# Layer 0 of a two-layer transformer: values' projection one unit later, two gate transposes earlier, and another order of the last two batches' normalisations and expert choices

## The chip, the cores and the metric

The kernel runs on one core of one Trainium2 chip. A core has five engines with a queue of instructions each: TensorE (PE in the profile, its weight loads PEld), VectorE (DVE), ScalarE (ACT), GpSimd (POOL) and SyncE (SP), which issues transfers. They wait for one another by semaphores. The metric is the device time of one execution in microseconds, lower is better; times shown are medians of several runs. The profile is one further execution; its times are counted from the start of its span.

## The reference, cut to what matters

Eight sequences (batches) of 256 tokens of 128 features pass through two layers. Each layer is an attention and a mixture of experts, both behind a normalisation that is modulated per sequence:

```
h = layernorm(x) * (1 + ca) + sa
x = x + ga * attention(h, W_qkv, b_qkv, W_out, b_out)     # 16 heads of 8, causal
h = layernorm(x) * (1 + cb) + sb
logits = h @ Wr                                           # 8 experts, the best 2 of each token
x = x + gb * (shared_ffn(h) + sum over the token's 2 experts of gate * expert_ffn(h))
```

The modulations (sa, ca, ga, sb, cb, gb) are linear in a small input. The shared feed-forward network and each expert have a hidden width of 512. Layer 1 is alike, with other sizes; the change touches layer 0 alone.

## The kernel before, in words

The order of the work is written out by hand: each engine runs its instructions in the order in which the program states them, and waits only on data and on buffers. Around the loops stand tables of steps: `at(n, ...)` puts a step into unit n ahead of its value products, `at_end(n, ...)` at the unit's end, and `at_head(n, half, ...)` behind the exponential of one of its two halves. Steps of one list run in the order in which they were registered.

**Attention of layer 0.** The loop runs over 24 units n = 3b + u, three for each batch b. `scores0(b, u)` (L1117, L1129) makes transposed scores on PE into two PSUM buffers "s", ACT takes their exponentials into `pt` (L1133), and for u = 0 and 1 POOL clears what lies above the diagonal (`causal`, L820). Two units later `values0` (L1151) multiplies `pt` with the values `vm`. In unit u = 1 the next batch is projected: `project0(b+1)` (L1081; ACT writes k and four scaled queries, L1084 and L1086) and `project_v0(b+1)` (vp on PE, L1095; the addition of the bias on DVE, L1098, writes `vm`). When a batch's three units are through, `normalise0(b)` (DVE, L1161 to L1171: transpose, reciprocal, multiplication, transpose back, giving aT) and, a unit later, `finish0(b)` (y on PE, L1184, added to x on DVE, L1187) close it.

All small products (qk, vp, y, nt, lg, rk, gp) share two PSUM buffers with the tag "p".

**Routing of layer 0.** It runs in six spans of batches, (0,1), (2,3), 4, 5, 6, 7, most of it inside the attention loop. For a span, `norm0` gives four steps: measure (statistics on DVE, L748 to L753, and a power on POOL, L754), normalise (xn on DVE, L764), modulate (nt on PE, L773; h on DVE, L782) and tokens (two multiplications on POOL, L1209 and L1210). `route0` is cut into steps as well: the logits lg (PE, L1231) and the best expert (DVE, L848 to L855); the second best and the counts (DVE, L848 to L912); the ranks rk (PE, L915 to L918) and the row numbers idx (DVE, L920 to L926); and then one scatter for each half batch and choice, so four for a batch (POOL, L930). A scatter writes 128 tokens into the experts' rows `xs` in DRAM. A small memset (L1388) stands ahead of each, in `scatter(go, times)`. The last scatter of all waits until all the others have landed and stands for them.

**The end of the stage.** After the loop a written-out list finishes batch 7, the routing of batches 5 to 7, and the shared network of the four wide tiles w (512 tokens each): `hides` are the hidden products (L1264, gelu on ACT, L1267), `projects` the outputs (ysh, L1288), four token groups for each w, of which the last product adds the experts' biases with the gates turned to rows (L1292). `turn_gates0(w)` makes those: a transpose on PE (gp, L1274) and a copy on DVE (gT, L1276). The gates of the first two wide tiles are computed in units 19 and 21. Then SyncE reads each expert's rows (`fetch_rows0`, xg, L1321), and 39 expert tiles follow (L1327 to L1350), for which POOL gathers weights by index (L1047).

Of the kernel before, what the change touches and what calls it, by code (L numbers as in the profile page):

```python
# [17 lines left out]
B, S = 8, 256  # L18
# [539 lines left out]
def fast_path(ctx: ExitStack, tc: tile.TileContext, i: dict, out: bass.AP, bad: bass.AP):  # L558
# [19 lines left out]
    def ps_ln(shape, name):  # L578
        return pp.tile(shape, F32, tag="p", name=name)
# [97 lines left out]
    def modulation(n):  # L677
        mp = ps_ln([P, 7, B], f"mp{n}")
        for k, what in enumerate((SA, CA, GA, SB, CB, GB)):
            nc.tensor.matmul(  # L680
                out=mp[:, what, :], lhsT=wmod[n][:, bass.ts(k, P)], rhs=silu_c[n], start=True, stop=True
            )
        m = md[n]
        nc.vector.tensor_copy(m[:, SA:, :], mp[:, SA:, :])
        nc.vector.tensor_scalar_add(m[:, CA, :], m[:, CA, :], 1.0)
        nc.vector.tensor_copy(m[:, 0:BG, :], mp[:, 0:BG, :])
# [116 lines left out]
    def batch_cols(tiles, b):  # L803
        return tiles[b * S // TW][:, bass.ds(b * S % TW, S)]

    def batch_tokens(b):
        return x[b // 2][:, bass.ts(b % 2, 2), :]
# [264 lines left out]
    SPANS0 = ((0, 2), (2, 2), (4, 1), (5, 1), (6, 1), (7, 1))  # L1072
# [18 lines left out]
    def project_v0(b):  # L1091
        hb = batch_cols(h, b)
        vp = ps_ln([P, 2, P], f"vp0_{b}")
        for j in range(2):
            nc.tensor.matmul(  # L1095
                out=vp[:, j, :], lhsT=hb[:, bass.ts(j, P)], rhs=wqkv[:, bass.ts(2, P)], start=True, stop=True
            )
        nc.vector.tensor_tensor(  # L1098
            vm[b % 3].rearrange("p k a (m c) -> p k (a m) c", m=2)[:, :, :, 0:D0],
            vp.rearrange("p k (h d) -> p k h d", d=D0),  # L1100
            bv.rearrange("p (h d) -> p h d", d=D0).unsqueeze(1).to_broadcast([P, 2, H, D0]), ALU.add,
        )
# [54 lines left out]
    def normalise0(b):  # L1157

        o = st0.pop(("o", b))
        ot = ap0.tile([P, 2, S // 32, 32], F32, tag="ot", bufs=1, name=f"ot0_{b}")  # L1160
        nc.vector.transpose(ot.rearrange("p s k c -> p (s k c)"), o.rearrange("p s q -> p (s q)"))  # L1161
        r = rs0[:, b]
        nc.vector.reciprocal(r, ot[:, :, :, 16:18])
        at = ap0.tile([P, S // 32, 2, 2, D0], F32, tag="t", name=f"at0_{b}")
        for s in range(2):
            nc.vector.tensor_tensor(
                at[:, :, s], ot[:, s, :, 0:16].rearrange("p k (m d) -> p k m d", m=2),
                r[:, s].unsqueeze(3).to_broadcast([P, S // 32, 2, D0]), ALU.mult,
            )
        aT = ap0.tile([P, S], F32, tag="aT", name=f"aT0_{b}")  # L1170
        nc.vector.transpose(aT, at.rearrange("p k s m d -> p (k s m d)"))  # L1171
        st0["aT", b] = aT
# [5 lines left out]
    def finish0(b):  # L1178
        aT = st0.pop(("aT", b))
        xb = batch_tokens(b)  # L1180
        shape = [P, 2, P]
        y = ps_ln(shape, f"y0_{b}")
        for j in range(2):
            nc.tensor.matmul(  # L1184
                out=y[:, j, :], lhsT=aT[:, bass.ts(j, P)], rhs=mdb0[:, GA - 1, b, :], start=True, stop=True
            )
        nc.vector.tensor_tensor(xb, xb, y, ALU.add)  # L1187
# [11 lines left out]
    def norm0(bs):  # L1199

        kept = []
        name = f"0b{bs[0]}"

        def tokens():
            b, half = bs[0] // 2 * 2, bs[0] % 2
            if not half:
                tokens0["all", b] = ap0.tile([P, 4, P], F32, tag="ht", bufs=2, name=f"ht{name}")
            ht = tokens0[bs] = tokens0["all", b][:, bass.ds(2 * half, 2 * bs[1]), :]
            nc.gpsimd.tensor_tensor(by_batch(ht), by_batch(kept[0]), rows_of_span(mdb0[:, CB - 1], bs), ALU.mult)  # L1209
            nc.gpsimd.tensor_tensor(by_batch(ht), by_batch(ht), rows_of_span(mdb0[:, SB - 1], bs), ALU.add)  # L1210

        first = 2 * (bs[0] % 2)
        return [
            *layernorm_parts(
                bs[0] // 2, md[0], SB, CB, name, ps_ln, lambda w, xn: kept.append(xn),
                range(first, first + 2 * bs[1]),
            ),
            tokens,
        ]

    def route0(bs):

        nt = 2 * bs[1]
        first = 2 * bs[0]
        ts = bass.ds(first, nt)
        name = f"0_{bs[0]}"
        shape = [P, nt, E0]
        lg = ps_ln(shape, f"lg{name}")
        for j in range(nt):
            c = bass.ts((first + j) % TT, P)  # L1230
            nc.tensor.matmul(out=lg[:, j, :], lhsT=h[bs[0] // 2][:, c], rhs=wr, start=True, stop=True)  # L1231
        s = z0.s12[:, ts]
        yield from top2_steps(ap0, lg, s, g12[:, ts], name, -1e30)
        yield from z0.place_steps(first, nt, lambda: tokens0[bs], ps_ln)
# [37 lines left out]
    def turn_gates0(w):  # L1272
        gp = ps_ln([P, P], f"gp0_{w}")
        nc.tensor.transpose(gp, gates[:, bass.ts(w, TT), :].rearrange("p j e -> p (j e)"), ident)  # L1274
        gT = hid0["g", w] = ap0.tile([P, P], F32, tag="gT", bufs=2, name=f"gT0_{w}")
        nc.vector.tensor_copy(gT, gp)  # L1276
# [97 lines left out]
    def at(n, *steps):  # L1374
        early.setdefault(n, []).extend(steps)

    def at_end(n, *steps):
        ends.setdefault(n, []).extend(steps)
# [5 lines left out]
    def one(steps):  # L1384
        return lambda: next(steps, None)

    def apart_on_gpsimd():
        nc.gpsimd.memset(most, P - 0.5)  # L1388

    def scatter(go, times):  # L1390
        for _ in range(times):
            apart_on_gpsimd()
            go()

    N0 = 3 * B
    at_end(3, lambda: modulation(1))
    at_end(4, lambda: normalise0(0))
    at_end(5, lambda: scale_wout(), lambda: add_bias(0), lambda: add_bias(1))
# [11 lines left out]
            at_end(n + 1, lambda w=w: add_bias(w))  # L1410
        at_end(n + 3, modulate)
    at(6, lambda: finish0(0))
    for b in range(1, B - 1):
        at_end(3 * b + 4, lambda b=b: normalise0(b))
        at_end(3 * b + 5, lambda b=b: finish0(b))
    ways = {}
    spots = {
        0: ((13, 1), (14, 0), (14, 0), (14, 1), (16, 1), (17, 0), (17, 0), (17, 1)),
        2: ((19, 1), (20, 0), (20, 0), (20, 0), (20, 1), (21, 0), (21, 1), (21, 1)),
        4: ((22, 1), (22, 1)), 5: (),  # L1420
    }
    for bs in SPANS0[:4]:
        n = 3 * sum(bs) + 2
# [12 lines left out]
    at_end(19, first_gates)  # L1436
    at(21, first_gates)
    norm6, norm7 = norm0(SPANS0[4]), norm0(SPANS0[5])
    at_end(23, norm6[0], lambda: ways[SPANS0[3]]())

    project0(0)
    project_v0(0)
# [12 lines left out]
    def set_up():  # L1455
        rd0 = rows_of(0, md[0])
        spread(mdb0, rd0, GA, 4)
        spread(gb0.unsqueeze(1), rd0, GB, 1)
        w1.update({n: load(w1p, n, nc.sync) for n in ("wo1", "gate_w", "wg1", "wu1", "wd1")})
        for n in range(2):  # L1460
            nc.sync.dma_start(out=wds1[bass.ts(n, I1), :], in_=i["wds1"])
        nc.sync.dma_start(out=gate_b, in_=i["gate_b"].partition_broadcast(P))
        nc.sync.dma_start(out=bp32, in_=i["bp32"])
        z0.clear(zero)
        z1.clear(zero)
        for e in range(E0 - 3):
            wst.append(ap0.tile([P, WPK], F32, bufs=1, name=f"wst{e}"))
            nc.sync.dma_start(out=wst[e], in_=i["wpk"][bass.ts(e, P), :])
        nc.gpsimd.memset(gates, 0.0)
        nc.gpsimd.memset(gates[:, :, E0 : E0 + 1], 1.0)  # L1470

    rd1 = []

    for n in range(N0):
        b, u = divmod(n, 3)
        scores0(b, u, behind.pop(n, {}))
        if n == 0:
            set_up()
        if u == 1 and b + 1 < B:
            project0(b + 1)  # L1480
            project_v0(b + 1)
        for step in early.pop(n, ()):
            step()
        if n > 1:
            values0(*divmod(n - 2, 3))
        for step in ends.pop(n, ()):
            step()


    go4, go5 = ways[SPANS0[2]], ways[SPANS0[3]]  # L1490
    go6, go7 = one(route0(SPANS0[4])), one(route0(SPANS0[5]))

    hides = [one(shared_hidden_steps0(w)) for w in range(3)]
    projects = [one(shared_project_steps0(w)) for w in range(3)]
# [5 lines left out]
    go5()  # L1500
    normalise0(B - 1)
    norm6[2]()
    scatter(go4, 2)
    scatter(go5, 4)
    for n in range(len(wst), E0):
        fetch_weights0(n)
    hides[0]()
    finish0(B - 1)
    norm7[0]()
    go6()  # L1510
    norm6[3]()
    norm7[1]()
    go6()
    turn_gates0(0)
    projects[0]()
    norm7[2]()
    go7()
    go6()
    scatter(go6, 4)
    projects[0]()  # L1520
    norm7[3]()
    go7()
    projects[0]()
    projects[0]()
    go7()
    scatter(go7, 4)
    hides[1]()
    last_gates()
    one(shared_add0(0))()
    turn_gates0(1)  # L1530
    hides[1]()
    for n in range(6):
        fetch_rows0(n)
# [517 lines left out]
    for n in range(N):  # L2051
        b, u = divmod(n, 4)
# [22 lines left out]
    go6, go7 = (one(route1((b, 1))) for b in (B - 2, B - 1))  # L2075
# [206 lines left out]
```

## Time and profile before

| What | Value |
|---|---|
| Time, median of 3 runs | 606.93 us (605.57 to 607.95) |
| The profiled execution: its time, its span | 603.21 us, 601.5 us |
| Mean granted TensorE clock | 0.967 |
| PE busy | 539.9 us (90%) |
| DVE, ACT, POOL busy | 330.9, 268.1, 263.0 us |
| Attention loop of layer 0, PE's first scores to its last y in the loop | 14.1 to 111.4 us |
| End of the stage: last scatter landed, first expert row turned on PE | 146.56, 150.41 us |
| First unit of layer 1's attention on PE | about 247 us |

Four views are used below. The chain that ended last follows the last instruction back to what released it, step by step; its lines give start, length and what ran, and "issue" is time in which the engine waited for nothing that the view shows. The waits give who waited for whom: microseconds in total, how often, the longest. The timeline gives the start and the length of an engine's instructions in order of time, merged where alike follow one another, with the idle time ahead of them and what ended it in brackets. The stage view gives each engine's busy time and the granted TensorE clock in a stretch of the span. [...]

### The profile page before, as it was taken

To read this page: it belongs to the slowest core of one execution; us is meant where nothing else is said; L and a number is where in the kernel's file an instruction comes from. 1 tells how busy PE (TensorE), PEld (TensorE's weight loads), DVE (VectorE), ACT (ScalarE), POOL (GpSimd) and SP (SyncE) were. 2 spreads that over 40 slices of the span, in tenths; PEclk is the share of its full clock that TensorE was granted. 3 is DMA by queue.
4 is the path that set the end of the run, shared out by engine and by line. 5 is a ranking of instruction groups with operands and counts; after the bars stand their busy time and mean duration, and the time that the engine had idled before them with its cause. 6 is when DMAs were issued, how large, how long until landed. Compare 5 with 4: busy or idle time off the path is not lost.

```text
span 601.5 us, 11911 instructions
## 1 busy us (share of the span) xinstructions
PE 539.9 (90%) x4443; PEld 383.3 (64%) x4443; DVE 330.9 (55%) x1005; ACT 268.1 (45%) x486; POOL 263.0 (44%) x404
## 2 busy tenths in 40 slices
PE   5998999867999999899999999999999989888960
PEld 4454454554999998666676767676766757764450
DVE  4257776864422222465535765655647495654693
ACT  3686666403455563275334442445262542522430
POOL 5323578846044442375612354633065553104750
PEclk9998999979899999899999999999999999888996
DMA  8799994402289992410403031300303036563441
GB/s 274 275 402 404 390 355 168 142 19 79 89 263 319 342 309 74 161 28 19 94 5 72 11 81 23 81 23 3 71 20 88 14 86 195 170 190 77 104 103 59
DMA packets 53567, 85.41 MB, mean 142 GB/s; under 512 B 6652, under 2 KB 32764, under 8 KB 52348
## 3 DMA queue, kind: packets, MB, share of 16 engines
q1 hardware_dynamic: 45308, 60.50, 31.5%
q0 software_dynamic: 8048, 23.67, 12.8%
q8 instruction: 37, 0.61, 0.4%
q10 hardware_dynamic: 144, 0.39, 0.2%
q14 instruction: 30, 0.25, 0.1%
HBM read 53.46 MB, written 31.07 MB: 141 GB/s over the span
## 4 chain that ended last, share of the span: by engine, by line
PE 60%; DVE 13%; DMA 10%; ACT 5%; issue 5%; POOL 5%; SPq 1%; POOLq 0%; DVEq 0%; ACTq 0%
PE sc L1641 7%; PE o L1663 6%; PE qp L1610 5%; PE hp L1336 5%; PE yt L1344 4%; PE kp L1610 4%; PE y L1716 4%; PE vp L1623 4%; PE sc L1117 4%; PE sum L1671 3%; DMA wt<-in_wpk_dram,widx 3%; POOL xs L930 3%; PE o L1151 2%; DMA xg<-xs 2%; ACT pt L1133 1%
## 5 line engine op out<-in xcount | busy, mean ns | idle before, releaser
L820 POOL TENSOR_SCALAR_AFFINE_SELECT pt<-pt 128x256 f32<-128x256 f32 (+1 forms) x144 | 67.2, 494 | 152.6 <-ACT pt L1644 116.3
L1055 POOL DMA_INDIRECT yg<-ys,yidx x56 | 54.3, 970 | 52.1 <-DMA ys<-ysb 34.0
L1644 ACT ACTIVATE pt<-sc 128x768 f32<-128x768 f32 x64 | 48.4, 808 | 25.8 <-PE sc L1641 25.7
L1133 ACT ACTIVATE pt<-sc 128x1024 f32<-128x1024 f32 x48 | 46.5, 1023 | 24.8 <-PE sc L1117 15.5
L1641 PEld LDWEIGHTS sc<-q,k 64*128 64x128 f32 x512 | 41.6, 187 | 18.8 <-issue 13.9
L1338 ACT ACTIVATE hst<-hp,wt 128x128 f32<-128x128 f32 x136 | 38.9, 368 | 29.7 <-ACT hst L1338 20.1
L1047 POOL DMA_INDIRECT wt<-in_wpk_dram,widx x31 | 29.0, 935 | 50.3 <-PE xT L1327 49.7
L1641 PE MATMUL sc<-q,k 64*128 64x256 f32 (+1 forms) x512 | 50.5, 336 | 0.0
L1663 PE MATMUL o<-pt,v 128*64 128x256 f32 (+1 forms) x512 | 49.0, 332 | 1.3 <-DVE ou L1675 1.3
L1626 ACT COPY v<-vp 128x512 f32<-128x512 f32 x32 | 18.8, 586 | 67.0 <-PE vp L1623 67.0
L1614 DVE COPY q<-qp 128x512 f32<-128x512 f32 x32 | 22.0, 688 | 39.9 <-PE qp L1610 39.9
L1663 PEld LDWEIGHTS o<-pt,v 128*64 128x64 f32 x512 | 32.0, 136 | 18.5 <-POOL pt L820 5.3
L1349 DVE COPY ysb<-yt 128x128 f32<-128x128 f32 x39 | 11.4, 292 | 54.9 <-PE yt L1344 54.9
L1610 PE MATMUL qp<-h,wq 128*128 128x256 f32 x128 | 36.8, 411 | 2.8 <-DVE q L1614 1.4
L930 POOL DMA_INDIRECT xs<-ht0b,idx x32 | 32.2, 1005 | 15.0 <-issue 12.0
L1336 PE MATMUL hp<-xTs,wt 128*128 128x128 f32 x272 | 36.7, 278 | 1.9 <-DMA wt<-in_wpk_dram,widx 1.4
L1117 PE MATMUL sc<-qm,k 32*128 32x512 f32 x192 | 35.9, 702 | 2.1 <-ACT pt L1133 1.5
L1623 PE MATMUL vp<-wv,h 128*128 128x512 f32 x64 | 36.1, 646 | 0.0
L1344 PE MATMUL yt<-wt,hst 128*128 128x128 f32 x272 | 35.8, 275 | 0.0
L1336 PEld LDWEIGHTS hp<-xTs,wt 128*128 128x128 f32 x272 | 33.0, 191 | 3.7 <-issue 1.6
L1610 PE MATMUL kp<-h,wk 128*128 128x256 f32 x128 | 33.7, 387 | 0.0
L1614 ACT COPY k<-kp 128x512 f32<-128x512 f32 x32 | 18.8, 588 | 33.3 <-PE kp L1610 33.3
(298 smaller groups left out, 1088.7 us busy)
## 6 DMA issues: line engine op xcount, KB each, us to landing
xs<-zero SPq DMA_DIRECT2D x1, 12288.0 KB, 58.3
xs<-zero SPq DMA_DIRECT2D x1, 8192.0 KB, 25.3
rb<-rd SPq DMA_DIRECT2D x14, 512.0 KB, 5.9
mdb<-mrd SPq DMA_DIRECT2D x2, 2048.0 KB, 7.3
xg<-xs SPq DMA_DIRECT2D x63, 64.0 KB, 3.0
wt<-in_wpk_dram SPq DMA_DIRECT2D x24, 128.0 KB, 2.6
wst<-in_wpk_dram SPq DMA_DIRECT2D x5, 514.0 KB, 12.4
ys<-ysb SPq DMA_DIRECT2D x10, 256.0 KB, 3.2
```

The costliest lines, as they stand in the source:

```text
L820: nc.gpsimd.affine_select(out=pt, in_=pt, compare_op=ALU.is_ge, fill=0.0, base=0, pattern=[[0, pt.shape[1]], [1, P]], channel_multiplier=-1,)
L930: self.apart(nc.gpsimd.indirect_dma_start(out=self.xs[:, :], out_offset=bass.IndirectOffsetOnAxis(ap=idx[:, j, k : k + 1], axis=0), in_=to ...
L1055: nc.gpsimd.indirect_dma_start(out=yg[:, k, :], out_offset=None, in_=self.ys[:, :], in_offset=bass.IndirectOffsetOnAxis(ap=self.yidx[:, j, ...
L1117: nc.tensor.matmul(out=sc[:, n, :].rearrange("p (a q) -> p a q", q=rhs.shape[2]), lhsT=k[r, cols], rhs=rhs, start=True, stop=u < 2,)
L1133: nc.scalar.activation(pt[:, bass.ts(half, 2), :], sc, AF.Exp)
L1336: nc.tensor.matmul(out=hp[:, c, :], lhsT=wt[:, bass.ts(c, P)], rhs=xT, start=True, stop=True)
L1344: nc.tensor.matmul(out=y, lhsT=hs[:, c, :], rhs=wt[:, bass.ds(WF + c * P, P)], start=(c == 0), stop=(c == FC - 1))
L1610: nc.tensor.matmul(out=ps_[:, n, :], lhsT=w1[f"w{what}1"][:, bass.ts(2 * u + n, P)], rhs=hb, start=True, stop=True)
L1623: nc.tensor.matmul(out=vp, lhsT=hb[:, bass.ts(j, P)], rhs=w1["wv1"][:, bass.ts(half, 512)], start=True, stop=True)
L1641: nc.tensor.matmul(out=sc[:, n, cols], lhsT=k[r, m, bass.ts(kb, P)], rhs=q[r, m, qs], start=True, stop=True)
L1644: nc.scalar.activation(pt, sc[:, :, 0:384], AF.Exp, scale=1.0 / math.sqrt(D1))
L1663: nc.tensor.matmul(out=o[bass.ts(n, D1), m, qs], lhsT=v[:, kb, bass.ts(4 * (u % 2) + 2 * m + n, D1)], rhs=pts[m][:, n, cols], start=(kb == ...
```

## The change

Four things differ in layer 0; the operations themselves, their sizes and their number are the same.

- The values of batch b are projected in its own first unit (n = 3b) instead of the unit 3b − 2. Queries and keys stay where they were.
- `normalise0(b)` and `finish0(b)` of batches 1 to 6 are registered first, so they lead the lists of units 7, 10 and 13 instead of standing behind the modulation's last steps and the addition of the bias.
- The gates of wide tiles 0 and 1 are turned at the end of unit 23, not within the shared network's products. All four scatters of batch 4 stand in units 22 and 23, not two of them.
- In the written-out end, batch 6's tokens come ahead of batch 5's scatters; batch 7's power stands ahead of the last of these; batch 6's choice, ranks and scatters come ahead of batch 7's modulation and choice; the shared network's outputs are spread between them in another way.

```diff
     N0 = 3 * B
+    for b in range(1, B - 1):
+        at_end(3 * b + 4, lambda b=b: normalise0(b))
+        at_end(3 * b + 5, lambda b=b: finish0(b))
     at_end(3, lambda: modulation(1))
...
     at(6, lambda: finish0(0))
-    for b in range(1, B - 1):
-        at_end(3 * b + 4, lambda b=b: normalise0(b))
-        at_end(3 * b + 5, lambda b=b: finish0(b))
     ways = {}
     spots = {
...
-        4: ((22, 1), (22, 1)), 5: (),
+        4: ((22, 0), (22, 1), (22, 1), (23, 0)), 5: (),
     }
...
-    at_end(23, norm6[0], lambda: ways[SPANS0[3]]())
+    at_end(23, norm6[0], lambda: turn_gates0(0), lambda: turn_gates0(1), lambda: ways[SPANS0[3]]())
...
         if u == 1 and b + 1 < B:
             project0(b + 1)
-            project_v0(b + 1)
+        if u == 0 and b:
+            project_v0(b)
...
     normalise0(B - 1)
     norm6[2]()
-    scatter(go4, 2)
-    scatter(go5, 4)
+    norm6[3]()
+    scatter(go5, 3)
     for n in range(len(wst), E0):
         fetch_weights0(n)
     hides[0]()
     finish0(B - 1)
     norm7[0]()
+    scatter(go5, 1)
     go6()
-    norm6[3]()
+    projects[0]()
+    go6()
     norm7[1]()
+    projects[0]()
     go6()
-    turn_gates0(0)
+    scatter(go6, 4)
     projects[0]()
     norm7[2]()
     go7()
-    go6()
-    scatter(go6, 4)
-    projects[0]()
-    norm7[3]()
-    go7()
-    projects[0]()
     projects[0]()
     go7()
+    norm7[3]()
+    hides[1]()
+    go7()
     scatter(go7, 4)
-    hides[1]()
     last_gates()
     one(shared_add0(0))()
-    turn_gates0(1)
     hides[1]()
```

## The prediction

> **What bounds the kernel now.** I read the chain that ended last first, then the waits of the two stretches that the change touches, then each engine's timeline there. "Unit n" is the n-th pass of the 24-pass attention loop; b is a batch. The chain shows that the end of layer 0's routing hangs on GpSimd's scatters:
>
> ```profile
> 123.94 0.05 POOL most L1388
> 123.99 7.45 issue
> 131.44 1.06 POOL xs L930
> ...
> 144.34 2.23 DMA xs<-ht0b,idx
> ...
> 147.43 6.11 DMA xg<-xs
> ```
>
> GpSimd (POOL) stands 7.45 us before batch 6's first scatter; then eight scatters follow, the last lands at 146.56, and only then SyncE may read the experts' rows (xg). What POOL waited for is VectorE's (DVE) row numbers, and behind what those stood, the timelines of DVE and PE tell:
>
> ```profile
> 122.48 1.57 DVE L764 TENSOR_SCALAR xn0b<-x,mv0b,rstd0b 128x128 f32<-128x128 f32 x2 [0.89 <-POOL rstd0b L754]
> ...
> 125.46 0.28 DVE L1276 COPY gT<-gp 128x128 f32<-128x128 f32 x1
> ...
> 130.50 0.17 DVE L926 CAST idx<-slot 128x4 int32<-128x4 f32 x1
> ```
>
> ```profile
> 125.80 0.79 PE L1292 MATMUL ysh<-bp,gT 128*128 128x128 f32 x2 [4.99 <-DVE gT L1276]
> ```
>
> A ring of in-order queues: batch 7's normalisation waits for POOL's power, which stands behind the last scatters of batch 5 (to 121.69); the gates' copy gT stands behind that on DVE; PE waits 4.99 us for gT; batch 7's transpose, its logits and batch 6's ranks (rk) stand behind that on PE; and idx6 behind all. In the attention, the chain from 41 to 52 us shows where DVE held PE:
>
> ```profile
> 43.26 0.42 DVE vm L1098
> 43.68 1.88 DVE xn0a L764 x4
> ...
> 46.33 0.60 DVE x L1176
> 46.93 0.64 DVE ot L1161
> ...
> 48.50 0.46 DVE aT L1171
> 48.96 0.14 issue
> 49.09 0.68 PE y L1184 x4
> 49.78 2.02 PE sc L1117 x8
> ```
>
> and the waits from 12 to 112 us show what the values' projection costs in unit 3b+1:
>
> ```profile
> PE y L1184 <- DVE aT L1171: 2.1, 2, 1.8
> ...
> PE nt0b L773 <- DVE vm L1098: 1.6, 3, 0.5
> ```
>
> (nt0b needs the PSUM buffer that vm's DVE addition empties.) From 94.6 to 123.98 POOL has no gap but the 0.2 us between scatters.
>
> [...]after 3.4 us with PE busy 1.57 (46.3 to 49.7) the clock is 0.51 to 53.2; after 0.00 (121.4 to 124.8) it is 0.51 to 131.7. [...]Here an xn instruction of 0.33 us took 1.21 beside a 1.09 us causal select.
>
> **The change, part by part.** Times are of the new kernel, worked from the durations of this trace.
>
> *Projection moved (vp, vm), seven times.* PE's work is the same: 0.46 us leave unit 3b+1 and enter unit 3b+3. Around the chain shown: the first batches end 0.4 late (vp1 and vp2 come before exponentials that ACT runs back to back), so PE ends unit 8's values at 47.75 instead of 47.27. But on DVE xn no longer stands behind vm3, and the normalisation of batch 1 comes before the modulation (0.77) and the bias addition (0.60): xn runs 43.5 to 44.65, its four steps (0.64+0.36+0.50+0.46, with gaps 2.05) end near 46.8, a microsecond before PE arrives. The 1.82 us wait goes; PE is then busy through that window, so I expect the half clock at 49.7 to go too (sc 2.02 to 1.07, o 1.68 to 1.00). Against that stands vp3 (0.46) and the second half of sc, held by ACT to 48.85. nt0a of unit 9 ends at 52.05 instead of 54.06: **2.0 gained**. Unit 10: no vp4 (0.46), no vm wait (0.52), and lg takes another buffer than ACT's (0.59 wait); now 3.5. Later units lose 0.46 at u=0, regain it at u=1, and save 0.28 (y3), two more vm waits of 0.52, and some 0.5 each where sc's second half was stretched by ACT in units 13, 15 and 19, because vp now gives ACT time. I put in 0.65 of loss in unit 19, where xn of batch 4 stands behind a causal select[...]. Sum at unit 22: **5.6 on PE**. POOL's causal select of unit 19 ends when its exponential does, 4.7 earlier: 89.95 instead of 94.67.
>
> *Four of batch 4's scatters inside units 22 and 23.* A scatter is 0.96 and 0.3 of memset and start: 1.27. Two more now stand before batch 6's power (pow6). From unit 19's select POOL stays full: pow6 ended 19.43 after it, and now 19.43 + 2×1.27 = 21.97 after, at 111.9 (before 114.10). The select of unit 22 has one scatter ahead, ends 105.8, and PE needs it at 106.4: no cost; with 0.6 less cover it would cost what is missing. Their DMAs (64 KB, landing after 2.2) meet a DMA share of 0.25 between 95 and 112 us, and no SyncE transfer waits for them but the rows, at the end.
>
> *Gates turned early.* Two PE transposes (0.33) and two DVE copies (0.28 each); the second transpose waits for a PSUM buffer that DVE empties at 106.3. They delay the values of unit 22 by some 0.5 on PE and batch 5's choice by 0.45 on DVE (to 109.7); both are covered by the wait for pow6 until 111.9, and cost 0.45 without it. What goes is the 4.99 wait.
>
> *Other order of batches 6 and 7.* From pow6 the DVE line decides: xn6 0.55, batch 5's rows 0.95 (idx5 at 113.45[...]), then as in the old trace from idx5 to batch 6's first choice (116.3 to 121.6: 5.3), second choice 1.6, xn7 0.6, rows 0.9: idx6 = idx5 + 8.4, **121.9 to 122.6 against 130.67**. pow7, behind three of batch 5's scatters (to 118.65), comes in time for xn7 at 120.5. PE: two ysh groups (1.25 each) come before rk6 and end at 119.3; rk6 waits for the second choice at 120.5, which is the same DVE line. ACT's order is unchanged; SP's and the weight gathers behind it on POOL keep theirs.
>
> *From idx6 to the rows.* Four scatters, tokens 1.55, four scatters, the last waiting for all to land: 146.56−130.67 = 15.9, unchanged. idx7, behind two ysh groups and half a hidden tile, is due about 128.6, before POOL is free at 129.7. **Rows readable at about 138.2 instead of 146.58: 8.3 gained.** PE's shared-expert work, 5 us of wait and the half clock less, ends about 138.5, before rows arrive (150.41−8.3 = 142.1), so it stays hidden.
>
> After that both kernels run the same expert tiles and layer 1. Sum for the profiled execution: span 601.5−8.3 = 593.2, its time 603.21−8.3 = 594.9. The median of the runs shown is 606.93, 3.7 above that execution; so 598.6, and I say **599**[...].
>
> [...]
>
> **Rivals.**
> (a) *Only the end gains.* POOL, not PE, sets the attention's last third; were unit 19's select no earlier, pow6 would end 94.67+21.97 = 116.65, idx6 at 126.7 to 127.4: 3.3 to 4 gained, about 603. For it: POOL has no gap after 94.6. Against: before it, POOL waits for ACT's exponentials (35.8 us in 13 waits), so it follows ACT and PE.
> (b) *The gain is eaten.* PE stands idle in the new end too (110.4 to 112.5 for xn6, 119.3 to 120.5 for the second choice). If that halves its clock from 111 to 118, the ring's own PE steps (nt6, y7, lg6, together 1.7) double[...].[...]
> (c) *Slower.* The moved vm stands in DVE's line at unit 3b+3, behind a PE projection that stands behind sc, which waits for ACT. DVE already waited 17.0 us for vp in 8 waits, then mostly idle; now ranks, norms and the y of batch b−2 are behind it. I find 0.8 (vm7) and 0.3 (vm3). It decides against the change if the waits come to about 1.6 in each of the seven units: 11 lost against 8 gained, 610.
> That the change does not do what it says (gT still late) would need the gates unfinished at unit 23; they are written at 106.3, before unit 22 ends.
>
> **How the numbers follow.** Forecast 0.66 (gain 6 to 10.5: 596.5 to 601); (a) 0.18 (601.5 to 604); (b) 0.10 (604 to 610); (c) 0.06. Half a per cent, 3.0 us, is about what a measurement of this kernel can tell from no change. Faster by more: 0.66 + 0.18 = 0.84; same 0.10; slower 0.06. Range 595 to 604: it leaves out (b), (c) and a gain above 12.
>
> **What would show it.** Right: no PE wait on aT near 47 us and no half clock at 50; no wait of nt0b on vm; no wait of ysh on gT; POOL's wait before batch 6's first scatter 2 to 3.5 us instead of 7.45; first xg read near 138. Wrong, if: DVE's waits for vp move others (c); pow6 ends after 114; PE is half-clocked between 111 and 122 (b); or the tiles after the rows take longer than 80 us between 160 and 240 in the old trace.

## The result, and the profile after

The changed kernel takes **599.75 us** (median of 4 runs, 598.55 to 601.0) against 606.25 us of the kernel before on the same chip (median of 4 runs, 603.41 to 607.95): ratio 0.9898, 95% interval 0.985 to 0.9946. Run again on another chip (the third of the experiments below), with 13 runs against 42, it took 599.38 us against 604.43: ratio 0.9928, interval 0.9896 to 0.9961. Both intervals hold ratios from 0.99 to 0.994, a gain of about 4 to 6 us. The forecast was 599.0.

The two runs left two traces of the changed kernel, and they differ; single executions of it spread from 595.6 to 603.4 us on that other chip, so a span is read with that in mind. Times are from the start of the span:

| What ends or starts, us | before | after | after, second trace |
|---|---|---|---|
| select of unit 19 ends on POOL | 94.67 | 92.04 | 91.94 |
| y of batch 6 starts on PE | 110.70 | 111.61 | 109.21 |
| batch 6's power (pow6) ends on POOL | 114.10 | 114.64 | 114.10 |
| idx6 written by DVE | 130.67 | 126.59 | 124.55 |
| first expert row turned on PE | 150.41 | 146.32 | 143.73 |
| that row to the last expert tile's output | 81.64 | 83.69 | 84.79 |
| span | 601.5 | 599.0 | 599.0 |

The forecast was worked out for such a profiled execution: 8.3 us less at the first row and a span of 593.2. Both traces miss that span by 5.8 us.

**The middle of the attention is what was forecast.** The chain that ended last, from 45 to 53 us of the kernel after, holds PE alone where the old one went through DVE's vm, xn, x, ot and aT:

```profile
45.67 1.14 PE sc L1117 x8
46.81 0.97 PE sc L1129 x4
47.78 1.00 PE o L1151 x16
48.78 0.64 PE y L1184 x4
49.43 1.40 PE sc L1117 x8
50.82 0.64 PE vp L1095 x4
51.47 1.00 PE o L1151 x16
52.47 0.59 PE nt0a L773 x4
```

The wait of 1.82 us for aT is gone, and with it the half clock at 50: from 49.7 to 53.2 us the granted clock is 1.00 where it was 0.51, and eight score products take 1.40 us instead of 2.02.

**In this trace the last third gives all of that back.** The same chain, from 100 to 108 us:

```profile
100.65 0.74 POOL rstd0b L754
...
101.41 0.60 DVE xn0b L764 x2
102.01 0.08 DVE g L1245
102.09 1.78 DVE g L1246
...
104.44 0.47 DVE h L782
104.91 0.04 issue
104.95 1.02 PE lg L1231 x4
105.97 2.02 PE sc L1117 x8
```

Batch 5's power stands behind batches 2 and 3's scatters and ends at 101.4; DVE's xn waits for it; a gate instruction of 128x8 elements takes 1.78 us; batch 5's h and logits are late, and the scores after them run at half speed (2.02 us for eight). The stage view gives PE's busy time and its granted clock there:

```profile
101.36:104.77 3.41, 1.50 (x34) 1.09 (x34) 3.29 (x7) 1.56 (x2) 3.06 (x6) 1.00 0.20 40
104.77:111.60 6.83, 6.65 (x32) 2.47 (x32) 4.29 (x12) 1.94 (x2) 6.06 (x11) 0.50 0.31 108
...
118.43:121.84 3.41, 1.95 (x14) 1.38 (x13) 2.90 (x8) 2.31 (x4) 2.77 (x5) 1.00 0.33 127
121.84:125.25 3.41, 3.41 (x19) 3.41 (x18) 2.93 (x19) 0.00 (x0) 2.35 (x5) 0.50 0.08 28
```

(Columns: stretch, its length, busy time of PE, PEld, DVE, ACT, POOL, granted PE clock, DMA share, GB/s.) PE is busy 1.50 of 3.41 us; for the next 6.83 us its granted clock is 0.50. Batch 6's y starts at 111.61, 0.9 later than before.

**The end is much as forecast.** POOL's timeline of the kernel after, and its chain at the end:

```profile
113.92 0.72 POOL L754 TENSOR_TENSOR rstd0b<-rstd0b,minus_half 128x2 f32<-128x2 f32 x1
...
126.86 0.96 POOL L930 DMA_INDIRECT xs<-ht0b,idx  x1 [2.10 <-DVE idx L926]
```

```profile
140.15 2.22 DMA xs<-ht0b,idx
142.39 3.80 DMA xg<-xs
...
146.32 0.66 PE xT L1327 x2
```

POOL waits 2.10 us ahead of batch 6's first scatter instead of 7.45, PE no longer waits for gT, and idx6 comes 11.95 us after pow6, not 16.57. The first row is turned 4.1 us earlier.

**In the second trace the chain runs over POOL.** From unit 19 to batch 4's last scatter at 112.3 it stays on that engine (pow6 stands next behind; the chain goes on by that scatter's landing to batch 5's idx on DVE, which waits 0.21 us for it):

```profile
94.42 0.73 POOL ht0b L1210
...
99.17 0.96 POOL xs L930
...
100.16 0.72 POOL rstd0b L754
...
107.00 1.10 POOL pt L820
...
109.61 0.96 POOL xs L930
```

Here the same gate instruction took less than a tenth of the time (VectorE's timeline, first the kernel's first trace, then its second):

```profile
101.41 0.60 DVE L764 TENSOR_SCALAR xn0b<-x,mv0b,rstd0b 128x128 f32<-128x128 f32 x2 [1.29 <-POOL rstd0b L754]
...
102.00 1.86 DVE L1246 TENSOR_SCALAR g<-thg 128x8 f32<-128x8 f32 x1
```

```profile
101.39 2.22 DVE L764 TENSOR_SCALAR xn0b<-x,mv0b,rstd0b 128x128 f32<-128x128 f32 x2
...
103.61 0.16 DVE L1246 TENSOR_SCALAR g<-thg 128x8 f32<-128x8 f32 x1
```

But the instruction ahead was the long one: xn of batch 5 takes 2.22 us instead of 0.60. In both traces the long one starts before POOL's select and ends behind it: g at 103.86, with the select's end at 103.79, and both pieces of xn at 103.61, with the select's end at 103.27. From the start of xn to the end of the gates it takes 3.0 us in both.

PE's half clock fell at 97.7 to 104.6 instead (granted clock 0.50, and 1.00 from 104.6 to 111.4), and batch 6's y started 2.4 us sooner; yet pow6 ended at 114.10, only half a microsecond sooner. So the chain read from the first trace is one of two that are nearly equally long: batch 6's variance, which pow6 needs, is ready 0.1 us before POOL's list comes to pow6 in the first trace, and 2.0 us before it in the second. The experiments had to tell which of them counts.

**After the rows a part of the gain goes.** The waits of PE from 140 to 235 us, before and after, hold this line (us in total, times, longest):

```profile
PE hp L1336 <- DMA wt<-in_wpk_dram,widx: 1.4, 4, 0.6
```

```profile
PE hp L1336 <- DMA wt<-in_wpk_dram,widx: 3.5, 3, 2.3
```

The expert tiles wait 2.1 us longer for their gathered weights, and last 2.05 us longer. Of 4.1 us at the first row, 2.0 are left at the last tile. In the second trace the tiles last 3.15 us longer, and the weights explain only 0.8 of it; but its one wait, 2.15 us up to 216.5, is followed by a half clock from 217.2 to 220.6 (mean granted clock 0.86 from 210 to 220 us and 0.97 from 220 to 230), and neither of the other two traces has one there (1.00 in both).

### The profile page after: what moved, and what is told of

It reads as the page before. It is cut to its first block, busy times and chain, and to the rows that moved or that the text cites. A ratio compares the mean times of both kernels' runs of the same rounds, so it can differ in the third digit from the quotient of the medians.

```text
span 599.0 us, 11910 instructions
## 1 busy us (share of the span) xinstructions
PE 540.0 (90%) x4443; PEld 382.4 (64%) x4443; DVE 334.6 (56%) x1005; ACT 267.7 (45%) x486; POOL 263.4 (44%) x404
## 4 chain that ended last, share of the span: by engine, by line
PE 65%; DVE 14%; DMA 8%; issue 3%; POOL 3%; ACT 3%; SPq 1%; DVEq 0%; POOLq 0%; ACTq 0%
PE sc L1640 7%; PE o L1662 6%; PE qp L1609 5%; PE y L1715 5%; PE hp L1336 5%; PE yt L1344 5%; PE vp L1622 4%; PE kp L1609 4%; PE sc L1117 4%; PE sum L1670 4%; DMA wt<-in_wpk_dram,widx 3%; PE o L1151 3%; PE qk L1081 2%; POOL xs L930 2%; DMA gp<-gd 1%
## 5 line engine op out<-in xcount | busy, mean ns | idle before, releaser
L1133 ACT ACTIVATE pt<-sc 128x1024 f32<-128x1024 f32 x48 | 46.6, 1026 | 25.5 <-PE sc L1117 15.9
L1344 PEld LDWEIGHTS yt<-wt,hst 128*128 128x128 f32 x272 | 33.0, 192 | 0.0
```

The lines of the kernel that those rows point to most:

```text
L1133: nc.scalar.activation(pt[:, bass.ts(half, 2), :], sc, AF.Exp)
L1344: nc.tensor.matmul(out=y, lhsT=hs[:, c, :], rhs=wt[:, bass.ds(WF + c * P, P)], start=(c == 0), stop=(c == FC - 1))
```

## The experiments

All are compared with the kernel before on the same chip. Four chips were used; on the second, the kernel before takes 628.77 us, on the third 604.43, on the fourth 604.24, so only ratios are set side by side between chips. "Rows" is the first expert row turned on PE; it is read from one trace, and two traces of the changed kernel lie 2.6 us apart in it, so the times decide what a part is worth.

### One part alone

Three runs each take one part into the kernel before. p_vp has only the values' projection moved:

```diff
             project0(b + 1)
-            project_v0(b + 1)
+        if u == 0 and b:
+            project_v0(b)
```

> The kernel before with the values' projection moved, and nothing else. Theory A (each part gives what was counted): the wait of PE for aT in unit 8 falls from 1.82 to about 0.4 us, because xn no longer stands behind vm but the modulation and the bias addition (1.37) still stand ahead; the three waits of nt0b on vm are gone; 2 to 4 us earlier at unit 19's causal select, and 1.5 to 4 us less in all. Theory B (only the written-out end counts[...]): within 1 us of before.

Measured: 625.55 us, ratio 0.9948 (0.9924 to 0.9972): 3.3 us less. The wait of nt0b on vm is gone; PE still waits 0.99 us for aT in unit 8, not 0.4. Rows 149.15.

p_order has only the three lines that register `normalise0` and `finish0` of batches 1 to 6 first.

> The kernel before with the normalisation and closing of batches 1 to 6 registered first, and nothing else. Theory A: aT of batch 1 is ready 1.4 us earlier, PE's wait in unit 8 is about 0.4 us instead of 1.82; if that keeps the clock from halving at 50 us another 1.6 us; 1 to 3 us less in all. Theory B: within 1 us of before.

Measured: 626.49 us, ratio 0.9965 (0.9943 to 0.9987): 2.2 us less. PE waits 0.46 us in unit 8. Rows 150.41.

p_end has only the four scatters in units 22 and 23, the gates turned in unit 23 and the new list of the end.

> The kernel before with the four scatters in units 22 and 23, the early gates and the new order of the end, and the attention otherwise as before. Theory A: the power of batch 6 ends 2.5 us later than before (116.6), the row numbers of batch 6 come at 126.7 to 127.4 instead of 130.67, the last scatter lands 3.3 to 4 us earlier, and the time falls by 3.3 to 4 us. Theory B (the end is the whole of it): 6 us less, as the changed kernel. No change, if the earlier rows meet other work of PE.

Measured: 625.27 us, ratio 0.9956 (0.9932 to 0.9981): 2.8 us less. Rows 150.14; batch 6's y starts at 115.50, 4.8 later than in the kernel before and behind products at half speed (32 value products at 109.54 take 1.94 us; in the changed kernel's first trace, at 102.33, they take 1.08), and the end wins that back: from pow6 (119.50) to idx6 (131.11) it takes 11.6 us, where the old order took 16.6. So the saving of the end is the new order's own, with the attention as before.

p_att, run later on the fourth chip, has the first two parts together:

```diff
     N0 = 3 * B
+    for b in range(1, B - 1):
+        at_end(3 * b + 4, lambda b=b: normalise0(b))
+        at_end(3 * b + 5, lambda b=b: finish0(b))
...
-            project_v0(b + 1)
+        if u == 0 and b:
+            project_v0(b)
```

> The kernel before with both attention parts (projection moved, batches' normalisation first), its scatters, gates and end as before. Parts alone gave 3.3 (projection) and 2.2 us (order). Theory A (their gains add until POOL is full at unit 19): 3.3 to 5.5 us less than before, and the change's end adds 0 to 3 to that in the whole change. Theory G also says: no more than about 3.5, since both reach the same POOL list at unit 19, whose causal select ends 2.0 to 3 us earlier than before.

Measured: 602.47 us, ratio 0.9979 (0.9959 to 0.9999): 1.3 us less, below the low end of theory A. Its unit-19 select ends at 92.22, 2.4 earlier than before, but its pow6 at 114.71, no earlier, and its rows at 151.03. So two parts that gave 3.3 and 2.2 alone give 1.3 together: what the attention gains does not reach the rows. POOL's timeline shows that POOL was not what held pow6 here:

```profile
113.99 0.72 POOL L754 TENSOR_TENSOR rstd0b<-rstd0b,minus_half 128x2 f32<-128x2 f32 x1 [2.34 <-DVE g L848]
```

It stood 2.34 us for batch 6's variance, whose y PE began only at 111.80, behind products at half speed from 105.1 to 111.8 (eight score products at 106.09 take 2.09 us). In p_vp, where eight of them take 1.14 at 105.34, pow6 ended at 112.47. Both are traces of one execution, and why the half speed falls in one and not in the other is not settled.

### Are the gates, or the scatters, what holds pow6?

The gates' arithmetic goes to the end of unit 22, behind batch 5's h, so that the instruction of 1.86 us no longer stands ahead of PE's gap of 1.55 us and the half clock (0.50) behind it:

```diff
-    at(21, first_gates)
+    at_end(22, first_gates)
```

On the second chip:

> The changed kernel with the second step of the first gates at the end of unit 22 instead of ahead of unit 21's products, so that batch 5's h no longer stands behind the gate instruction that took 1.86 us beside GpSimd. Theory C ([...]this takes back the 5 us that the attention had won by unit 20): h of batch 5 about 1.8 us earlier, clock whole or half for one window less, y of batch 6 ends at 108 to 110 instead of 112.3, and the time 1.5 to 3.5 us below the changed kernel (a ratio of 0.983 to 0.988 to before). Rival D (GpSimd is full there and sets the end anyway): power of batch 6 ends at 114.6 as in the changed kernel, and the ratio stays at 0.990.

Measured: 619.63 us, ratio 0.9859 (0.9805 to 0.9914). That pointed to C, but the changed kernel was not beside it. So it was run again beside the changed kernel, with two of batch 4's scatters taken back behind pow6, and with both edits:

```diff
-        4: ((22, 0), (22, 1), (22, 1), (23, 0)), 5: (),
+        4: ((22, 1), (22, 1)), 5: (),
...
     norm6[3]()
+    scatter(go4, 2)
     scatter(go5, 3)
```

> The changed kernel itself, once more, as the standard for the three runs beside it, on one chip. Ratio to before 0.985 to 0.995. Its trace should show what its first trace showed: the gates' small DVE instruction held to well over 1 us beside POOL's scatter, PE standing over 1 us ahead of batch 5's logits, then the half clock, the end of y of batch 6 near 112.3, first xT near 146.3.

> The changed kernel with the first gates' arithmetic at the end of unit 22 instead of within unit 21. Theory C (the gates' small DVE instructions stand ahead of batch 5's h[...]; PE's gap and with it the half clock come partly from this): y of batch 6 ends 1.5 to 2.5 us earlier than in the changed kernel beside it, rows 1 to 2 us earlier, time 1 to 2.5 us less. Theory D (the difference to the changed kernel seen before is one between chips): the same within 0.6 us.

> The changed kernel with two of batch 4's four scatters back behind batch 6's power, all else as changed. Theory P (POOL is full from unit 19 on, so each scatter ahead of the power delays it by its 1.27 us, and batch 6's tokens and row numbers after it): power ends 2 to 2.5 us earlier, at about 112, the two scatters fill POOL's gaps behind it (1.6 us ahead of the tokens, 2.1 us ahead of batch 6's first scatter), rows 1.5 to 2.5 us earlier, time 1.5 to 2.5 us less. Theory Q (only POOL's total up to the last scatter counts, and the two only change places): power 2 to 2.5 us earlier but rows and time the same within 0.6 us.

> The changed kernel with both edits: the first gates at the end of unit 22, and two of batch 4's scatters behind batch 6's power. If C and P hold and are independent: 2.5 to 5 us less than the changed kernel, ratio to before 0.978 to 0.984. If POOL alone sets the end (P without C): as with the scatters alone. If D and Q hold: the same as the changed kernel.

| Kernel | median, us | ratio to before | pow6 ends | rows |
|---|---|---|---|---|
| changed (after_again) | 599.38 | 0.9928 (0.9896 to 0.9961) | 114.10 | 143.73 |
| gates late | 599.51 | 0.9920 (0.9891 to 0.9949) | 114.06 | 144.25 |
| two scatters back | 599.41 | 0.9899 (0.9872 to 0.9926) | 114.02 | 145.58 |
| both | 598.75 | 0.9906 (0.9869 to 0.9944) | – | – |

(For the last kernel no trace is used.)

Side by side the four cannot be told apart. D holds and C falls: the gate instruction's 1.86 us, so plain in the first chain, cost nothing that these runs can measure. (In the late place one of the gates' instructions was long again, 1.76 us at 106.3, with no loss in time that can be told.) What was expected of the changed kernel's second trace failed as well, as shown above: the gate took 0.16 us and the first row came at 143.7. P falls, and Q too in its mechanism: with two scatters less ahead of it, pow6 is not earlier at all. POOL's timeline of that kernel says why:

```profile
113.30 0.72 POOL L754 TENSOR_TENSOR rstd0b<-rstd0b,minus_half 128x2 f32<-128x2 f32 x1 [2.08 <-DVE rstd0b L753]
```

POOL now stands 2.08 us for batch 6's variance, which follows batch 6's y, late by PE's half speed (eight score products at 105.66 take 2.09 us there). So pow6 has two limits, 0.1 and 2.0 us apart in the two traces of the changed kernel: POOL's list and PE's late attention. Taking one away uncovers the other. The other traces fit: in all eight traces of kernels with four of batch 4's scatters ahead of pow6, those of the kernels below among them, POOL comes to pow6 without a wait; in p_vp, p_order, p_att and this one, with two, it waits 0.4 to 2.3 us for batch 6's variance (in the kernel before it does not).

### Work taken from POOL

Four of the eight scatters of batches 2 and 3 are left out; their rows stay zero, so the kernel does not compute those tokens' experts.

```diff
                     yield
+                    if self.tag == "0" and n == 1 and 2 * j + k in (1, 2, 6, 7):
+                        continue
```

> The changed kernel with four of the eight scatters of batches 2 and 3 left out (two ahead of batch 5's power, two behind the next causal select), so those rows stay zero: POOL has 4 x 1.27 = 5.1 us less to do between unit 19 and batch 6's power. Theory G (from unit 19 on POOL's own list sets batch 6's power, and PE's waits and half clock there are not what counts): batch 6's power ends 3 to 5 us earlier than the 113.4 to 113.9 of the changed kernel, rows and time 3 to 5 us less. Theory H (PE sets it, through batch 5's late logits and the half clock): the power waits for batch 6's attention instead; that moves only by what batch 5's power came earlier, 2.5 us, and rows and time by 0 to 2.5 us.

Measured: 592.11 us, ratio 0.9779 (0.9731 to 0.9828). POOL's powers for batches 5 and 6 in its timeline:

```profile
97.43 0.72 POOL L754 TENSOR_TENSOR rstd0b<-rstd0b,minus_half 128x2 f32<-128x2 f32 x1
...
108.40 0.73 POOL L754 TENSOR_TENSOR rstd0b<-rstd0b,minus_half 128x2 f32<-128x2 f32 x1
```

Pow6 ends at 109.13, 5 us earlier; 1.3 of that was there at unit 19's select (90.66), and from the select to pow6 it takes 18.5 us instead of 22.2 to 22.6. Batch 5's power is 3 us earlier, PE's longest gap there is 1.25 us, and from 97 to 118 us its products do not run at half speed (eight score products at 102.35 take 1.14 us). Rows at 139.41. Less POOL work moves both limits at once: batch 6's y starts at 105.40, earlier than H said, and POOL still comes to pow6 last, 0.8 us after the variance is ready. So G holds in pow6, but the run does not part POOL from PE: with batch 5's power earlier, PE's wait for it (1.02 us in the first trace) and the half speed went too. The rows are 4.3 to 6.9 us earlier than in the two traces of the changed kernel. The time falls by 7 to 9 us more than the changed kernel's, by the ratios, so more than G's 5; the tiles, with 0.2 us of wait for weights, last only 79.8 us.

A second try only moved POOL's scatters, so that batch 5's power came two of them sooner:

```diff
-        2: ((19, 1), (20, 0), (20, 0), (20, 0), (20, 1), (21, 0), (21, 1), (21, 1)),
-        4: ((22, 0), (22, 1), (22, 1), (23, 0)), 5: (),
+        2: ((19, 1), (20, 0), (20, 0), (21, 0), (21, 1), (21, 1), (22, 1), (22, 1)),
+        4: ((22, 1), (22, 1), (23, 0), (23, 0)), 5: (),
```

> The changed kernel with batch 5's power two scatters earlier on POOL (and the scatters of batches 2 to 4 pushed back), POOL's list up to batch 6's power the same in sum. Theory G: PE's wait ahead of batch 5's transposes goes and y of batch 6 ends 2 us or more earlier, yet batch 6's power stays within 0.7 us and the time within 1 us. Theory H: power, rows and time 2 to 4 us less.

Measured: 599.46 us, ratio 0.9902 (0.9867 to 0.9937), beside the fourth chip's other runs. It tells less than it should: the scatters stood behind unit 22's select, and POOL stood idle for it.

```profile
106.50 1.09 POOL L820 TENSOR_SCALAR_AFFINE_SELECT pt<-pt 128x1024 f32<-128x1024 f32 x1 [2.49 <-ACT pt L1133]
```

Pow6 came at 117.35, 3 us later, and rows at 147.13; the half speed fell at about 99 to 104.3 (sixteen value products at 100.44 take 1.94 us, at 108.54 they take 1.07). Neither theory foretold that. The time is still that of the changed kernel, within the interval.

### A long multiplication in unit 16

Why does unit 19's select end at 92.0 and not at 89.95? A candidate lies in unit 16. There the timelines of the kernel after show DVE's multiplication of the attention's output beside POOL's multiplication of the tokens of batches 2 and 3:

```profile
80.09 2.39 DVE L1166 TENSOR_TENSOR at<-ot,rs 128x128 f32<-128x128 f32 x2
```

```profile
80.83 1.28 POOL L1209 TENSOR_TENSOR ht0b<-xn0b,mdb 128x512 f32<-128x512 f32 x1
82.19 1.42 POOL L1210 TENSOR_TENSOR ht0b<-ht0b,mdb 128x512 f32<-128x512 f32 x1
```

```profile
86.50 0.18 PE L915 MATMUL rk<-marks,before 128*128 128x32 bf16 x1 [0.88 <-DVE x L1187]
```

The first of DVE's two pieces takes 2.19 us and ends at 82.27, when POOL's first multiplication has ended (82.11); the choice and x stand behind it, and PE waits 0.88 us ahead of the ranks. In unit 19 of the same trace the two pieces take 0.49 us together (at 92.39). The test moves POOL's two instructions behind unit 18's select:

```diff
-        at(n + 2, modulate, tokens)
+        at(n + 2, modulate)
+        at(n + 4 if bs[0] == 2 else n + 2, tokens)
```

> The changed kernel with POOL's two multiplications of the tokens of batches 2 and 3 behind unit 18's causal select, not in unit 16. Theory L (they hold VectorE's multiplication of the attention's output, 2.40 us for two instead of 0.5 to 0.74, and so batch 4's ranks, and PE 0.88 us ahead of them): the two take 0.5 to 0.8, PE's wait ahead of the ranks goes, unit 19's causal select ends 0.7 to 1 us earlier, and what follows with it: time 0 to 1 us less. Rival (the 2.40 us has another cause): it stays above 2.

DVE's timeline of this kernel:

```profile
78.97 0.49 DVE L1166 TENSOR_TENSOR at<-ot,rs 128x128 f32<-128x128 f32 x2
```

0.49 us instead of 2.39, and PE's wait for x is gone: L holds in this. A scatter beside it is not enough: in both traces the multiplication starts 0.32 us after the start of one, and only ahead of POOL's multiplication does it take 2.39. From the scores of unit 17 to those of unit 19 PE takes 6.59 us instead of 7.63, so 1.0 is gained there. The select ends at 90.63, 1.4 us earlier, but the edit did not win that: the scores of unit 17, ahead of all that it touches, already start 1.1 earlier (78.97 for 80.08), and only 0.3 comes after them, because the select now stands behind POOL's moved multiplications (86.96 to 89.59). Pow6 ends at 112.52, rows at 141.97; from 79 to 118 us PE's products do not run at half speed (eight score products at 103.38 take 1.14 us).

Time 597.06 us (595.37 to 597.35), ratio 0.9861 (0.9829 to 0.9894): 8.4 us less than before, more than was foretold. It is faster than the kernel before for certain. Its interval lies below that of the changed kernel on the third chip, and overlaps that on the first; but the changed kernel was not run beside it, and x_gates_late, whose first ratio was as low, did not keep its lead once it was. So a lead over the changed kernel (2 to 4 us by the ratios) is not settled, and 0.3 us at the select would not explain it.

## Why the prediction was right, and where not

The time was right (599.75 for 599.0), the size of the gain too large: 8.3 us were forecast at the rows, and 4.1 and 6.7 are seen there; 4.4 to 6.2 remain in the time. That the time is met within 0.75 us is in part luck: the forecast started from a median of 606.93, the kernel before then had 606.25, and the gain of the medians, 6.5, is at the upper end of what the two ratios allow.

1. **Projection and order, units 8 to 10.** Right in kind: no wait on aT, no half clock at 50, no wait of nt0b on vm. In size half: nt0a of unit 9 ends at 53.06, so 1.0 us is gained there and not 2.0. The missing 1.0 was lost ahead of unit 8, whose values end at 48.78 where 47.75 was said; from there to nt0a it takes the forecast 4.3. In the first trace PE's products took about twice as long until about 26 us, in the kernel before until about 22, while the stage view gives a granted clock of 1.00 there in both (the same four score products, after and before):

```profile
24.39 1.89 PE L1129 MATMUL sc<-masked,before 128*128 128x512 bf16 x4
```

```profile
23.88 1.04 PE L1129 MATMUL sc<-masked,before 128*128 128x512 bf16 x4
```

Four later traces with the same attention (x_gates_late, x_gates_late2, x_scatter_back, x_drop4) began y of batch 1 at 47.3 to 47.9, the first trace at 48.78. So this loss belongs to the executions, not for certain to the change. By y of batch 5 (94.70 for 99.31) the gain is 4.6, near the 5.6 forecast for unit 22.

2. **"POOL's causal select of unit 19 ends … 4.7 earlier".** The step that failed: it ends 2.6 earlier. Of the missing 2.1, 1.0 is the one of item 1. In the four traces without that loss the select ends at 90.66 to 91.22, 3.5 to 4.0 earlier, so 0.7 to 1.3 is missing there too, and two terms of the sum come to about as much. The loss of 0.65 that I put into unit 19 was an estimate; what the trace shows is DVE's multiplication of 2.19 us in unit 16, for which PE waited 0.88. And the select follows the start of unit 19's scores, 87.71 for 90.33, while part of what unit 19 saves on PE (vp 0.54, the wait on vm 0.52) comes behind that start: the gain grows from 2.6 there to 4.6 at y of batch 5, by 2.0, where the forecast took only 0.9 off PE's sum for the select.

3. **Scatters inside units 22 and 23.** The term was right: pow6 ends 22.6 and 22.2 us after the select, where 21.97 was said. So the attention's gain at the select (2.6) was spent on two more scatters (2×1.27), and pow6 ends where it did before: 114.64 and 114.10 for 111.9, which meets the forecast's own sign of being wrong, "pow6 ends after 114". This is rival (a)'s place, POOL in the last third, reached half way. That the two scatters cost 2.54 is right only while POOL is the limit: taken back, they freed nothing, because batch 6's y was as late.

4. **Gates early.** Right in the main: the 5.0 us wait is gone. Their cost is not covered everywhere: from the start of y of batch 6 to the values behind it PE takes 1.48 us instead of 0.64, and in the first trace that lies on the way to batch 5's ranks, for which DVE waited (item 5). Moving the gates' arithmetic shows no difference in time, whether a gate instruction takes 1.86 us, 1.76 or 0.16.

5. **The end's order.** Right: from pow6 to idx6 it took 16.57 us, and takes 11.95 and 10.45; 10.0 to 10.7 were forecast. The 1.5 by which the first trace is longer lies ahead of idx5, batch 5's row numbers: 3.76 us after pow6 in the first trace, 2.31 in the second, 1.55 to 2.3 by the forecast. Batch 5's ranks follow y of batch 6 on PE by 5.18 us in both traces; in the first, y came 2.4 later, behind the half clock from 104.8 to 111.6, and DVE stood 0.91 us for the ranks. From idx5 to idx6 both take the same, 8.2 and 8.1 (8.4 forecast). So the half clock at 121.8 to 125.3, in which eight products of the shared network take 1.71 us instead of 0.99, cost nothing on this path. The earlier one is of the kind that rival (b) feared, but ahead of the stretch that (b) named, and in one of two executions; that PE's idle time in the end would bring one was (b)'s estimate.

6. **From idx6 to the rows.** Right: the last scatter lands 15.8 and 15.1 us after idx6, for 15.9.

7. **"After that both kernels run the same expert tiles."** They do, but not in the same time: 83.69 and 84.79 us instead of 81.64, with PE waiting 3.5 and 2.2 us for gathered weights instead of 1.4. I had held this stage fixed. The waits alone do not make up the second trace's 3.15; the half clock at 217.2 to 220.6, behind its one long wait, adds up to 1.7 by an estimate from the mean granted clocks (0.14 and 0.03 of 10 us). Over the traces of all kernels, that wait is 0.2 to 2.6 us (mean 1.3) in the five whose rows come after 149 us, and 0.2 to 5.8 (mean 2.6) in the nine with earlier rows. What makes a gather late was not tried and stays open; x_drop4, with the earliest rows, waits 0.2.

Rival (c) did not come about: p_vp, which has the moved vm alone, is faster, not slower.

So the two errors, pow6 (2.2 forecast, nothing gained) and the tiles (nothing forecast, 2 to 3 lost), both cost time, and the range held because the largest piece, the ring at the end (6.1 of 8.3; 4.6 and 6.1 measured), was read well. p_end, which has that order with the old attention, shows the same saving, 5.0.

## What to carry to other kernels

Where an in-order engine's list has no gap, time gained ahead of it is spent on that list (2.6 us at unit 19's select, none at pow6): move work off it before speeding up what feeds it, and look which second limit then comes up (here POOL's scatters and PE's attention, late by the half clock, lay at most 2 us apart, and neither of the two single edits gave anything that can be told). Where an instruction of one engine grows long ahead of one of another (2.39 us for two pieces that take 0.49 elsewhere), move one of the two to where its engine has slack, and look what the moved one now stands ahead of: one such move, of two instructions on POOL, took 1.0 us off PE's way, and 0.3 of it reached POOL's select. Read two traces of one kernel before a single long instruction or a single stretch of half clock is made the cause. And compare stretches that start from the same event: of the 1.4 us by which that select came earlier, 1.1 were there before the edit could act.

## What the runs showed of the hardware

- One and the same instruction (128x8, DVE) took 0.16 us in one execution and 1.86 in the other of the same kernel, beside a scatter and a select on POOL. In the execution with 0.16 the instruction ahead of it was long (xn's two pieces of 128x128, 2.22 us for 0.60). Both had started during the scatter, 0.7 to 0.8 us before the select; g ended 0.07 after it and xn's second piece 0.34. The first piece of the multiplication in unit 16 started 0.74 before POOL's multiplication and ended 0.16 after it (2.19 us). In x_tok18, beside a scatter that a memset followed, both pieces together took 0.49.
- In the first trace of the changed kernel the granted clock was 0.50 from 104.77 to 111.60, from 121.84 to 125.25 and from 145.73 to 152.57; in the second it was 0.50 from 97.74 to 104.57 and 1.00 from 104.57 to 111.40. What PE was busy in the stretch ahead of a half clock differs: 44% (101.36 to 104.77), 57% (118.43 to 121.84) and under 1% (142.30 to 145.73) in the first trace, 69% (94.30 to 97.74) in the second, while after 56% in the first (203.75 to 207.17) the clock stayed 1.00. So no single share of busy time, as the records give it, divides them.
